# A third tile for the mixed rows, and exponentials built one channel at a time, in a kernel of a 3x3 convolution and a Laplace layer

## The chip, the cores and the metric

The kernel runs on one core of one Trainium2 chip. The metric is the device time of one execution in microseconds (us), taken as the median of several runs. Everything is float32.

## The reference

Input x has 16 images of 16 channels of 256 x 256. Two layers follow one another, each as x + L(norm(x)), where norm is a group norm over 8 groups of two channels without weights:

```python
x = x + conv3x3_circular(group_norm(x))          # written with FFTs in the reference
x = x + laplace(group_norm(x))

# laplace(x), per batch b, input channel i, output channel k:
alpha = fft2(x)
A  = 1 / (omega1 - pole1)        # [freq_y, i, k, 4]
Bm = 1 / (omega2 - pole2)        # [freq_x, i, k, 4]
S  = einsum('ikpq,oikp,xikq->oxik', residue, A, Bm)
x1 = ifft2(einsum('biox,oxik->bkox', alpha, S)).real
D  = einsum('biox,oikp,xikq->bikpq', alpha, A, Bm)
r2 = einsum('bikpq,ikpq->bkpq', D, residue)
E1, E2 = exp(pole1 * ty), exp(pole2 * tx)
x2 = einsum('kbpq,bipz,biqx->kizx', r2, E1, E2).real
return x1 + x2 / (256 * 256)
```

What matters below are the mixing (for each frequency pair a 16 x 16 complex matrix S takes the channels of alpha to the channels of the result) and the exponentials E1 and E2.

## The kernel before

The work runs in four stages, one after the other on one core.

1. *Convolution* (to about 595 us): statistics of x, the 3x3 convolution as small matmuls on TensorE (PE), and on the side the tables of A for the y frequencies (among them ct, by way of cD in HBM).
2. *Spectrum* (to about 1195 us): each image is folded along y and x and transformed by matmuls; the result goes to aD in HBM, and projections of it (D) are summed in proj.
3. *Mixing* (to about 1870 us), the stage that the change is about.
4. *Back transform* (to the end): loads of mixed rows (yk), matmuls along x and y, the transient x2 added, and the sum written out.

**The mixing loop** (lines 1222 to 1245) has 32 passes g of four steps n. One pass handles four x frequencies; its mixing matrices are in a tile sg of 32 KB per partition, of which there are two, so that pass g mixes with one while the other is filled for g + 1. A step does, in this order:

- `sums(n, w_now)`: 32 small matmuls that build a quarter of the next pass's matrices from ct and the weight tile w (line 1032), into two of four PSUM banks.
- a new tile yt (line 1228) from the pool `yp`, which has two buffers of 8 KB.
- `spread`: two copies on ScalarE (ACT, line 1049) and two shuffles on VectorE (DVE, line 1052) from PSUM to the next sg.
- four times `mix` (line 1120): 16 matmuls into one PSUM bank, and its eviction to yt (line 1233), three on ACT and one on DVE, or two and two in the step after one in which the exponentials put work on ACT.
- `store` (line 1134): four DMAs of 128 KB from yt to yD in HBM; and `load` (lines 1102, 1107): none, four, four and four DMAs (of 256 KB for n = 1, half of these ahead of the store) that bring the next pass's rows of aD into the tiles abd, which the step has just used up. All of them are issued by SyncE (SP).
- one step of `weights(g + 2)` (line 895): DVE builds v in three steps, and at n = 2 GpSimd (POOL) makes the weight tile w from it (line 930). The sums of the next pass's step 0 are the first to read it.
- one step of the generator `exps` (from g = 1 on).

All of it is emitted inside `tc.manual_schedule()`: every engine issues its instructions in the order in which they are written here. A tile of a pool that lands on bytes of an earlier tile waits for the users of those bytes (`reuse_waits="tile"`), and so does a new tile for the users of the one whose buffer it takes.

**The exponentials** (`make_exps`, lines 1161 to 1214) come in 16 pairs of channels, 8 for E1 and 8 for E2. A pair takes seven steps of the generator, with tiles of 128 x 512 (2 KB per partition), one buffer each: s_th, s_rn, s_tmp and s_ex. On POOL: the products of time and pole (two instructions of 256), then the reduction to one turn (three instructions for rn at lines 1181 to 1184, and three times a product in s_tmp and a subtraction, lines 1190 and 1191), then two that clamp. ACT makes the exponential into s_ex at the end of the third step and the sine in the fifth; POOL multiplies and folds in the sixth; SP stores s_ex to eD in the seventh.

```python
for c in (c1, c2, c3):
    nc.gpsimd.tensor_scalar(tmp, rn, float(c), None, ALU.mult)
    nc.gpsimd.tensor_tensor(th, th, tmp, ALU.subtract)
    if c == c2:
        yield
```

Ahead of the loop `first_sums` fills the first sg, and `finish_projections` turns the projections into o2 with the constant jmat. In the last pass (g = 31) there are no sums; `unmix_first` mends the rows of frequency 0 in HBM, and the first loads of stage 4 wait for the stores.

The functions that the change touches follow.

Of the kernel before, what the change touches and what calls it, by code (L numbers as in the profile page):

```python
# [9 lines left out]
FP = mybir.dt.float32  # L10
AF = mybir.ActivationFunctionType
ALU = mybir.AluOpType
# [4 lines left out]
B = 16  # L17
C = 16
N = 256
P = 128  # L20
PI = float(np.pi)
# [3 lines left out]
def conv_then_laplace_kernel(ctx: ExitStack, tc: tile.TileContext, a: dict, out: bass.AP):  # L25
# [15 lines left out]
    nc = tc.nc  # L41
    x = a["x"]

    cp = ctx.enter_context(tc.tile_pool(name="const", bufs=1))
# [6 lines left out]

    later_loads = []

    def const(name, shape):
        t = cp.tile(shape, FP, name=name, tag=name)
        later_loads.append((t, a[name]))
        return t

    cols = const("cols", [P, 24])
    kmask = const("kmask", [P, C])  # L60
    fold2 = const("fold2", [P, 2, 64])
    o2 = cp.tile([P, B, 2, 16], FP, name="o2", tag="o2")
    proj = cp.tile([P, 2, B, 16, 2], FP, name="proj", tag="proj")
    jmat = cp.tile([P, 3, P], FP, name="jmat", tag="jmat")

    def pitched(name, rows, row, *split):

# [5 lines left out]
    for b in range(B // 4):  # L73
        t = dp.tile([P, C, 8 * N + 256], FP, name=f"vD{b}", tag=f"vD{b}")
# [20 lines left out]

    ptab = ExitStack()
    tp = ptab.enter_context(tc.tile_pool(name="tables", bufs=1))
    vmr = tp.tile([P, 2, B, C], FP, name="vmr", tag="vmr")


# [54 lines left out]
    own = m16[:, 0:C:2]  # L155
    load_consts()
    halves[1] = [load_x(1, h) for h in range(2)]
    nc.sync.dma_start(out=jmat, in_=a["jmat"])
    ones = tp.tile([P, P], FP, name="ones", tag="ones")
    nc.vector.memset(ones, 1.0)  # L160
    tiny = wp.tile([P, 8], FP, name="tiny", tag="tiny")
# [557 lines left out]
    def pool(stage, name, bufs=1, **kw):  # L719
        return stage.enter_context(tc.tile_pool(name=name, bufs=bufs, reuse_waits="tile", **kw))  # L720
# [11 lines left out]
    u0 = pool(p1, "u0")  # L732
# [151 lines left out]
    m0, m1, nm0 = cols[:, 0:1], cols[:, 1:2], cols[:, 9:10]  # L884
# [10 lines left out]
    def weights(g):  # L895

        shape = [P, 32, 4]
        u = up["u" if g else "u0"].tile([P, 4, 32, 4], FP, name="u", tag="u")  # L900
        w, den, e, f = (u[:, j] for j in range(4))
        pr2, pre, pim = (prU[:, j].unsqueeze(2).to_broadcast(shape) for j in range(3))
        nc.vector.tensor_tensor(
            w,
            omg[:, g].unsqueeze(1).to_broadcast(shape),
            pims.unsqueeze(2).to_broadcast(shape),
            ALU.subtract,
        )
        nc.vector.tensor_tensor(den, w, w, ALU.mult)
        nc.vector.tensor_tensor(den, den, pr2, ALU.add)  # L910
        yield
        nc.vector.reciprocal(den, den)

        nc.vector.scalar_tensor_tensor(e, w, m1, pre, ALU.mult, ALU.add)
        nc.vector.scalar_tensor_tensor(f, w, nm0, pim, ALU.mult, ALU.add)
        yield
        v = up["v"].tile([P, 32, 2, 4], FP, name="v", tag="v")
        nc.vector.tensor_tensor(v[:, :, 0], e, den, ALU.mult)
        nc.vector.tensor_tensor(v[:, :, 1], f, den, ALU.mult)
# [10 lines left out]
        nc.gpsimd.tensor_tensor(  # L930
            w4,
            v2.unsqueeze(2).to_broadcast(full),
            m4.unsqueeze(1).unsqueeze(3).to_broadcast(full),
            ALU.mult,
        )
        return wt
# [7 lines left out]
    for u in range(len(units) + 1):  # L944
        at = units[u] if u < len(units) else None
        if at is not None:
            now = vq
            t = lp.tile([P, 2, 4, 3, P], FP, name="t", tag="t")
# [32 lines left out]
    ptab.close()  # L981


    yp = pool(p2, "yt", 2)
    g0 = pool(p2, "sg0")
    a0 = pool(p2, "abd0")
    wp = pool(p2, "w", 2)
    ep = pool(p2, "exps")
    up["u"] = pool(p2, "u")
    a1 = pool(p2, "abd2")  # L990
    zp = pool(p2, "between")
    tp = pool(p2, "ct")
    a2 = pool(p2, "abd3")
    g1 = pool(p2, "sg1")
# [10 lines left out]
        z.tile([P, 4, 4, 16, B], FP, name=f"abd{j}", tag=f"abd{j}") for j, z in ((2, a1), (3, a2))  # L1005
    ]

    zp.tile([P, 384], FP, name="between", tag="between")
# [45 lines left out]
    def first_sums():  # L1054
# [27 lines left out]
            load(0, jq)  # L1082
        return sg, w1

    def finish_projections():


        for ro in range(2):
            ps = pm.tile([P, B, 16], FP, name="ps_o", tag="ps_mix")
            nc.tensor.matmul(ps, lhsT=jmat[:, 0], rhs=accs[:, ro], start=True, stop=False)  # L1090
            nc.tensor.matmul(ps, lhsT=jmat[:, 2 - ro], rhs=accs[:, 1 - ro], start=False, stop=True)
            nc.vector.tensor_copy(o2[:, :, ro], ps)

    def load(g, jq, rows=range(4)):

# [65 lines left out]
    def make_exps(which):  # L1161


        pl = ep.tile([P, C, 2], FP, name="s_pl", tag="s_pl")
        nc.sync.dma_start(out=pl, in_=a[f"pole_e{which + 1}"])
        t = ep.tile([P, N], FP, name="s_t", tag="s_t")
        nc.sync.dma_start(out=t, in_=a[("ty", "tx")[which]].to_broadcast([P, N]))
        sign, phase, turns = (cols[:, 2 + 3 * which + j : 3 + 3 * which + j] for j in range(3))
        pim = ep.tile([P, C], FP, name="s_pim", tag="s_pim")
        for _ in range(4):  # L1170
            yield
        nc.gpsimd.tensor_scalar(pim, pl[:, :, 1], sign, None, ALU.mult)
        for q in range(8):
            th = ep.tile([P, 2, N], FP, name="s_th", tag="s_th")
            rn = ep.tile([P, 2, N], FP, name="s_rn", tag="s_rn")
            tmp = ep.tile([P, 2, N], FP, name="s_tmp", tag="s_tmp")
            ex = ep.tile([P, 2, N], FP, name="s_ex", tag="s_ex")
            for j in range(2):
                i = 2 * q + j
                nc.gpsimd.tensor_scalar(th[:, j], t, pim[:, i : i + 1], None, ALU.mult)  # L1180
            nc.gpsimd.tensor_scalar(rn, th, 1.0 / (2 * PI), turns, ALU.mult, ALU.add)
            magic = 1.5 * 2.0**23
            nc.gpsimd.tensor_scalar(rn, rn, magic, None, ALU.add)
            nc.gpsimd.tensor_scalar(rn, rn, magic, None, ALU.subtract)
            yield
            c1 = 6.28125
            c2 = float(np.float32(1.93500518798828125e-3))
            c3 = 2 * np.pi - c1 - c2
            for c in (c1, c2, c3):
                nc.gpsimd.tensor_scalar(tmp, rn, float(c), None, ALU.mult)  # L1190
                nc.gpsimd.tensor_tensor(th, th, tmp, ALU.subtract)
                if c == c2:
                    yield
            nc.gpsimd.tensor_scalar(th, th, phase, 3.1415925, ALU.add, ALU.min)
            nc.gpsimd.tensor_scalar(th, th, -3.1415925, None, ALU.max)
            for j in range(2):
                i = 2 * q + j
                nc.scalar.activation(ex[:, j], t, AF.Exp, scale=pl[:, i, 0:1])
            yield True
            yield  # L1200
            nc.scalar.activation(th, th, AF.Sin)
            yield True
            nc.gpsimd.tensor_tensor(th, th, ex, ALU.mult)
            for op, eo in ((ALU.add, 0), (ALU.subtract, 1)):
                nc.gpsimd.tensor_tensor(
                    ex[:, :, eo * P : eo * P + P], th[:, :, 0:P], th[:, :, N - 1 : P - 1 : -1], op
                )
# [11 lines left out]
    finish_projections()  # L1219
    unmix = None  # L1220
    exps, late = chain(make_exps(0), make_exps(1)), None
    for g in range(32):
# [33 lines left out]
    ep = pool(p3, "et")  # L1256
# [3 lines left out]
    up = pool(p3, "ud", 2)  # L1260
# [150 lines left out]
    u = combine(0, yk, 1)  # L1411
# [12 lines left out]
    for n, (k, b0) in enumerate(units):  # L1424
# [9 lines left out]
        if n + 1 < len(units):  # L1434
# [3 lines left out]
            u = combine(units[n + 1][1], yk)  # L1438
# [171 lines left out]
```

## Time and profile before

| what | us |
|---|---|
| median of 3 runs | 2617.32 |
| the runs | 2607.34, 2626.05, 2617.32 |
| the profiled execution | 2623.94 |
| its span in the trace | 2622.1 |
| PE busy, share of the span | 2468.6, 94% |
| DVE busy | 1980.8, 76% |
| ACT busy | 1432.6, 55% |
| POOL busy | 1290.5, 49% |
| mixing loop, first sums (1218.09) to the last pass (1835.10) | 617.0 |

All times in the views are counted from the start of the span. A row of a timeline has start, duration, engine, line, operation, tile written and read, shapes, how many instructions are merged into it, and in brackets the idle time of the engine before it and what ended that. A row of a group has line, engine, operation, tiles and shapes, then busy us and mean ns of one, then the idle time before them and its causes. PE stands for matmuls, PEld for the loading of weights beside them.

### The profile page before, as it was taken

Reading aid. Unit: us, or ns where it says so; the run is one execution under the profiler, and the core shown is the slowest. Engines: PE = TensorE matmul, PEld = TensorE weight load, DVE = VectorE, ACT = ScalarE, POOL = GpSimd, SP = SyncE. Lnnn points to the kernel's source line nnn. Section 1 sums busy time; section 2 is a strip of 40 time slices with the busy share of each in tenths; the row PEclk is TensorE's granted clock in tenths of the full one; section 3 lists DMA queues with packets and bytes.
Section 4 is the critical chain, followed back from the end, with each engine's and each line's share of the span. In section 5 each row is a group of like instructions: output and inputs, shape, how many; then the busy total and the mean of one; then the engine's idle time right before and its main releaser. Section 6 shows DMA issues by size and latency. Waiting matters only on the chain.

```text
span 2622.1 us, 84262 instructions
## 1 busy us (share of the span) xinstructions
PE 2468.6 (94%) x35314; PEld 1885.3 (72%) x35314; DVE 1980.8 (76%) x3772; ACT 1432.6 (55%) x2599; POOL 1290.5 (49%) x1179
## 2 busy tenths in 40 slices
PE   5998999989999999998999999999799999999998
PEld 2444455567777777775878778788688888888887
DVE  7777788848888888887877878887276676667666
ACT  2565566666666666665666656666244444444443
POOL 1333378433333333333666645766555565555553
PEclk9999999989999999999999999999899999999999
DMA  7888878854655655655777777777988888888884
GB/s 274 276 279 282 294 270 294 297 211 177 240 195 209 242 220 194 245 225 190 225 229 214 226 225 222 222 227 228 253 302 289 291 292 279 299 289 287 291 287 174
DMA packets 318011, 653.17 MB, mean 249 GB/s; under 512 B 49174, under 2 KB 163990, under 8 KB 305728
## 3 DMA queue, kind: packets, MB, share of 16 engines
q1 hardware_dynamic: 316464, 640.57, 72.4%
q8 instruction: 278, 4.55, 0.7%
q0 software_dynamic: 896, 3.02, 0.4%
q10 hardware_dynamic: 272, 4.19, 0.4%
q14 instruction: 101, 0.83, 0.1%
HBM read 368.15 MB, written 280.36 MB: 247 GB/s over the span
## 4 chain that ended last, share of the span: by engine, by line
PE 58%; DVE 7%; DMA 4%; SPq 3%; ACT 3%; POOL 2%; issue 1%; ACTq 0%; DVEq 0%; POOLq 0%
PE ps_mix L1120 9%; PE ps_y L777 9%; PE ps_y L785 8%; PE ps_p L1361 7%; PE ps_f L1385 7%; PE ps_f L1386 7%; PE ps_x L820 5%; DMA yD<-yt 4%; PE ps_s L1032 2%; SPq L1134 2%; PE ps_h L1345 2%; PE psd L805 1%; DVE r L1394 1%; DVE ol L1396 1%; DVE ol L1397 1%
## 5 line engine op out<-in xcount | busy, mean ns | idle before, releaser
L1120 PE MATMUL ps_mix<-abd,sg 128*64 128x128 f32 x8192 | 482.2, 276 | 39.4 <-DMA yD<-yt 16.6
L1120 PEld LDWEIGHTS ps_mix<-abd,sg 128*64 128x64 f32 x8192 | 451.9, 138 | 92.9 <-ACT yt L1233 55.7
L1325 POOL TENSOR_TENSOR u<-yk 128x512 f32<-128x512 f32 (+1 forms) x268 | 358.2, 1369 | 314.7 <-PE ps_p L1361 249.1
L305 PE MATMUL ps_conv<-xt,wc 32*32 32x512 f32 x12288 | 445.6, 602 | 36.0 <-issue 26.1
L305 PEld LDWEIGHTS ps_conv<-xt,wc 32*32 32x32 f32 x12288 | 251.1, 103 | 217.6 <-issue 127.0
L793 ACT ACTIVATE t<-ps_y,vmr 128x384 f32<-128x384 f32 x512 | 297.1, 580 | 161.1 <-PE ps_y L785 161.1
L1052 DVE STREAM_SHUFFLE sg<-ps_s 128x512 f32<-128x512 f32 (+1 forms) x264 | 329.1, 1316 | 0.0
L777 PE MATMUL ps_y<-tabE,vq 128*128 128x256 f32 x1024 | 313.2, 388 | 11.0 <-DVE vq L766 9.4
L785 PE MATMUL ps_y<-tabO,vq 128*128 128x256 f32 x1024 | 305.9, 380 | 0.0
L275 POOL TENSOR_TENSOR pair<-pair,far 128x1024 f32<-128x1024 f32 x64 | 151.7, 2370 | 304.1 <-DVE pair L272 207.7
L1385 PE MATMUL ps_f<-pt,inv 128*128 128x256 f32 x1008 | 300.4, 380 | 0.0
L1386 PE MATMUL ps_f<-hs,ey 128*128 128x256 f32 x1008 | 299.8, 379 | 0.0
L1361 PEld LDWEIGHTS ps_p<-inv,u 128*128 128x128 f32 x2048 | 268.9, 193 | 35.4 <-POOL u L1329 10.9
L1389 DVE TENSOR_TENSOR r<-ps_f,q 128x256 f32<-128x256 f32 x256 | 107.0, 418 | 241.9 <-ACT q L1388 241.9
L1361 PE MATMUL ps_p<-inv,u 128*128 128x128 f32 x2048 | 276.2, 278 | 9.8 <-POOL u L1329 9.7
L1049 ACT ACTIVATE sg<-ps_s,mcol 128x512 f32<-128x512 f32 (+1 forms) x264 | 179.3, 689 | 192.2 <-DVE sg L1052 117.1
L777 PEld LDWEIGHTS ps_y<-tabE,vq 128*128 128x128 f32 x1024 | 189.6, 191 | 87.5 <-ACT q L833 51.2
L1388 ACT COPY q<-ps_f 128x256 f32<-128x256 f32 x256 | 95.4, 373 | 274.7 <-PE ps_f L1386 250.4
L1363 ACT COPY pt<-ps_p 128x512 f32<-128x512 f32 x256 | 151.5, 592 | 134.9 <-PE ps_p L1361 134.9
L765 POOL TENSOR_TENSOR vq<-vf 128x512 f32<-128x512 f32 x64 | 81.4, 1272 | 291.6 <-DVE vf L769 281.5
L785 PEld LDWEIGHTS ps_y<-tabO,vq 128*128 128x128 f32 x1024 | 195.4, 191 | 26.9
L1233 ACT COPY yt<-ps_mix 128x512 f32<-128x512 f32 x352 | 184.1, 592 | 55.8 <-DMA yD<-yt 42.2
(237 smaller groups left out, 3993.6 us busy)
## 6 DMA issues: line engine op xcount, KB each, us to landing
xt<-in_x SPq DMA_DIRECT2D x288, 258.0 KB
vD<-pair SPq DMA_DIRECT2D x256, 256.0 KB
yD<-yt SPq DMA_DIRECT2D x512, 128.0 KB
vl<-vD SPq DMA_DIRECT2D x128, 512.0 KB
out_y<-ol SPq DMA_DIRECT2D x128, 512.0 KB
s<-vD SPq DMA_DIRECT2D x126, 512.0 KB
aD<-spec SPq DMA_DIRECT2D x15, 4096.0 KB
yk<-yD SPq DMA_DIRECT2D x60, 1024.0 KB
```

The lines of the kernel that those rows point to most:

```text
L305: nc.tensor.matmul(acc[r][32 * c : 32 * c + 32], lhsT=ready[b][0][rows, phase, tap], rhs=halves[b][u // 2][rows, q : q + 5 : 4, 2 - tap : ...
L777: nc.tensor.matmul(ps[:, 0:N], lhsT=vf[:, xo, 0, j], rhs=tabE[:, 0 : i + 2 : i + 1], start=True, stop=False, skip_group_check=True,)
L785: nc.tensor.matmul(ps[:, P : P + N], lhsT=vf[:, xo, 1, j], rhs=tabO[:, i : C + 1 : C - i], start=False, stop=True, skip_group_check=True,)
L793: nc.scalar.activation(t[:, xo, j].rearrange("p l n -> p (l n)"), ps[:, 0:384], AF.Copy, scale=vmr[:, 0, b0 + j, i : i + 1],)
L1049: nc.scalar.activation(to[..., k : k + 2], src[odd], AF.Copy, scale=nsgn)
L1052: nc.vector.stream_shuffle(to[..., C + k : C + k + 2], src[1 - odd], swap)
L1120: nc.tensor.matmul(ps[64 * t : 64 * t + 64, j], lhsT=sg[:, f : f + 2].rearrange("p f m -> p (f m)"), rhs=abd[jq][:, :, 2 * t + cc, 2 * jj ...
L1233: (nc.vector.tensor_copy if m >= (2 if late else 3) else nc.scalar.copy)(o, src)
L1325: nc.gpsimd.tensor_tensor(u[:, :, j].rearrange("p b (c n) -> p c b n", c=8), in0, in1, o)
L1361: nc.tensor.matmul(ps[:, at], lhsT=u[:, n], rhs=tab, start=True, stop=True)
L1385: nc.tensor.matmul(ps[:, e], lhsT=tab, rhs=pt[:, e], start=True, stop=False)
L1386: nc.tensor.matmul(ps[:, e], lhsT=ey[:, e], rhs=hs, start=False, stop=True)
```

## The change

It gives yt a third buffer of 8 KB, and finds the room for it in other tiles:

- s_rn and s_tmp shrink to 128 x 256 (1 KB each). The reduction therefore runs for one channel of the pair after the other, with nine instructions each instead of nine for both; the first two steps of the generator now hold one channel each, and all three products of c1, c2 and c3.
- In `weights`, f is written over w, so that u has three parts instead of four.
- o2 is made in the bytes of proj; jmat is loaded at the start of the mixing stage into the buffer of s_ex; kmask and fold2 move to the pool of the tables, which is given up after stage 2; the empty tile "between" of the mixing stage goes.

```diff
-    o2 = cp.tile([P, B, 2, 16], FP, name="o2", tag="o2")
-    jmat = cp.tile([P, 3, P], FP, name="jmat", tag="jmat")
...
+    kmask = const("kmask", [P, C], tp)
+    fold2 = const("fold2", [P, 2, 64], tp)
...
-    nc.sync.dma_start(out=jmat, in_=a["jmat"])
...
-        u = up["u" if g else "u0"].tile([P, 4, 32, 4], FP, name="u", tag="u")
-        w, den, e, f = (u[:, j] for j in range(4))
+        u = up["u" if g else "u0"].tile([P, 3, 32, 4], FP, name="u", tag="u")
+        w, den, e = (u[:, j] for j in range(3))
...
-        nc.vector.scalar_tensor_tensor(f, w, nm0, pim, ALU.mult, ALU.add)
+        nc.vector.scalar_tensor_tensor(w, w, nm0, pim, ALU.mult, ALU.add)
...
-    yp = pool(p2, "yt", 2)
+    yp = pool(p2, "yt", 3)
...
-    zp = pool(p2, "between")
...
+    jmat = ep.tile([P, 3, P], FP, name="jmat", tag="s_ex")
+    nc.sync.dma_start(out=jmat, in_=a["jmat"])
+
     def finish_projections():
+        o2 = cp.tile([P, B, 2, 16], FP, name="o2", tag="proj")
...
             th = ep.tile([P, 2, N], FP, name="s_th", tag="s_th")
-            rn = ep.tile([P, 2, N], FP, name="s_rn", tag="s_rn")
-            tmp = ep.tile([P, 2, N], FP, name="s_tmp", tag="s_tmp")
+            rn = ep.tile([P, N], FP, name="s_rn", tag="s_rn")
+            tmp = ep.tile([P, N], FP, name="s_tmp", tag="s_tmp")
             ex = ep.tile([P, 2, N], FP, name="s_ex", tag="s_ex")
             for j in range(2):
                 i = 2 * q + j
                 nc.gpsimd.tensor_scalar(th[:, j], t, pim[:, i : i + 1], None, ALU.mult)
-            nc.gpsimd.tensor_scalar(rn, th, 1.0 / (2 * PI), turns, ALU.mult, ALU.add)
             magic = 1.5 * 2.0**23
-            nc.gpsimd.tensor_scalar(rn, rn, magic, None, ALU.add)
-            nc.gpsimd.tensor_scalar(rn, rn, magic, None, ALU.subtract)
-            yield
...
-            for c in (c1, c2, c3):
-                nc.gpsimd.tensor_scalar(tmp, rn, float(c), None, ALU.mult)
-                nc.gpsimd.tensor_tensor(th, th, tmp, ALU.subtract)
-                if c == c2:
-                    yield
+            for j in range(2):
+                z = th[:, j]
+                nc.gpsimd.tensor_scalar(rn, z, 1.0 / (2 * PI), turns, ALU.mult, ALU.add)
+                nc.gpsimd.tensor_scalar(rn, rn, magic, None, ALU.add)
+                nc.gpsimd.tensor_scalar(rn, rn, magic, None, ALU.subtract)
+                for c in (c1, c2, c3):
+                    nc.gpsimd.tensor_scalar(tmp, rn, float(c), None, ALU.mult)
+                    nc.gpsimd.tensor_tensor(z, z, tmp, ALU.subtract)
+                yield
```

More of the change, by code (lines that the diff above doesn't have):

```diff
@@ L52, in conv_then_laplace_kernel, with const @@
     later_loads = []
-    def const(name, shape):
-        t = cp.tile(shape, FP, name=name, tag=name)
+    def const(name, shape, home=cp):
+        t = home.tile(shape, FP, name=name, tag=name)
         later_loads.append((t, a[name]))
@@ L59, in conv_then_laplace_kernel @@
     cols = const("cols", [P, 24])
-    kmask = const("kmask", [P, C])
-    fold2 = const("fold2", [P, 2, 64])
-    o2 = cp.tile([P, B, 2, 16], FP, name="o2", tag="o2")
     proj = cp.tile([P, 2, B, 16, 2], FP, name="proj", tag="proj")
-    jmat = cp.tile([P, 3, P], FP, name="jmat", tag="jmat")
     def pitched(name, rows, row, *split):
@@ L918, in weights @@
         nc.vector.tensor_tensor(v[:, :, 0], e, den, ALU.mult)
-        nc.vector.tensor_tensor(v[:, :, 1], f, den, ALU.mult)
+        nc.vector.tensor_tensor(v[:, :, 1], w, den, ALU.mult)
         if g == 0:
@@ L1006, in conv_then_laplace_kernel @@
     ]
-    zp.tile([P, 384], FP, name="between", tag="between")
     ct = tp.tile([P, 4, 8, N], FP, name="ct", tag="ct")
@@ L1092, in finish_projections @@
             nc.vector.tensor_copy(o2[:, :, ro], ps)
+        return o2
     def load(g, jq, rows=range(4)):
@@ L1218, in conv_then_laplace_kernel @@
     ahead, wt = first_sums()
-    finish_projections()
+    o2 = finish_projections()
     unmix = None
```

## The prediction

> **What bounds the kernel now.** I read the busy lines of the page first, then its chain (section 4), then the stretches. The change acts in the mixing stage alone, from about 1195 to 1870 us; there the chain names ps_mix matmuls (9%), "DMA yD<-yt" (4%) and SP's issues of that store (2%). So I cut out the loop, from its first sums at 1218.09 to the first matmul of the last pass (g = 31) at 1835.10: 617.0 us for 31 passes of 4 steps. Busy times in nearly that stretch (us, then PE, weight loads, DVE, ACT, POOL, clock, DMA share, GB/s):
>
> ```profile
> 1226.00:1835.00 609.00, 578.20 (x11746) 490.05 (x11742) 493.21 (x881) 396.84 (x662) 378.32 (x288) 0.99 0.77 224
> ```
>
> PE is busy 95%, POOL only 62%, DMA 77%. An average hides what matters here, so next comes PE's timeline. Undisturbed, a step (32 sums, 64 mixing matmuls) takes 4.67 us; the third start below is 0.11 us late. The last row is a step that waited 3.17 us for a store, and ran slowly after it:
>
> ```profile
> 1751.86 1.09 PE L1032 MATMUL ps_s<-ct,w 64*32 64x256 f32 x32
> 1752.88 3.71 PE L1120 MATMUL ps_mix<-abd,sg 128*64 128x128 f32 x64
> 1756.64 1.10 PE L1032 MATMUL ps_s<-ct,w 64*32 64x256 f32 x32
> ...
> 1378.35 6.64 PE L1120 MATMUL ps_mix<-abd,sg 128*64 128x128 f32 x64 [3.17 <-DMA yD<-yt]
> ```
>
> The floor of the loop is 124 steps x 4.67 = 579.1 us; 37.9 us are lost. The waits between 1215 and 1850 us (total, times, longest) say to what:
>
> ```profile
> POOL w L930 <- DVE v L919: 188.2, 24, 17.9
> ACT yt L1233 <- DMA yD<-yt: 31.9, 27, 4.0
> PE ps_mix L1120 <- DMA yD<-yt: 16.6, 12, 3.2
> PE ps_mix L1120 <- DMA abd<-aD: 2.8, 3, 2.1
> ```
>
> So nearly all of the loss is the slot of yt that is still being stored. POOL's 188 us of waiting for DVE look like room; two further timelines say how much there is. POOL, around one weight tile w (L930) and the next:
>
> ```profile
> 1734.54 1.89 POOL L930 TENSOR_TENSOR w<-v,mcol 128x1024 f32<-128x1024 f32 x1 [5.58 <-DVE v L919]
> 1736.41 1.83 POOL L1180 TENSOR_SCALAR s_th<-s_t,s_pim 128x256 f32<-128x256 f32 x2
> 1738.35 0.69 POOL L1181 TENSOR_SCALAR s_rn<-s_th,cols 128x512 f32<-128x512 f32 x1
> ...
> 1751.14 2.01 POOL L1194 TENSOR_SCALAR s_th<-s_th,cols 128x512 f32<-128x512 f32 x1
> 1753.23 1.49 POOL L1195 TENSOR_SCALAR s_th<-s_th 128x512 f32<-128x512 f32 x1
> 1754.69 1.89 POOL L930 TENSOR_TENSOR w<-v,mcol 128x1024 f32<-128x1024 f32 x1
> ```
>
> In this pass POOL has no idle time: one pair of exponentials runs from 1736.41 to 1754.72, and w follows at once. w ends at 1756.58, and the sums that need it start at 1756.64. POOL is full in such a pass. SP, in a stretch in which PE waits for nothing:
>
> ```profile
> 1565.88 2.53 SPq L1107 DMA_DIRECT2D abd<-aD  x4
> 1568.52 3.15 SPq L1134 DMA_DIRECT2D yD<-yt  x4
> ...
> 1587.79 2.73 SPq L1134 DMA_DIRECT2D yD<-yt  x4
> 1590.62 1.23 SPq L1102 DMA_DIRECT2D abd<-aD  x2
> ```
>
> From 1565.88 to 1590.62 SP issues 36 transfers with no pause, 0.687 us each. The loop has 31 x 28 of them and 24 for the exponentials, 892, which is 613 us at this rate: SP is as full as PE, and the stores are late because their issues are.
>
> **The skill against the trace.** Two pages bear on this. The Trainium skill, "GPSIMD Engine Reference", section 3.1, says that each GpSimd instruction pays a dispatch in software beside its work per element; section 4.1 calls one-input work roughly line-rate. The trace (mean ns) agrees with the first and not with the second:
>
> ```profile
> L1191 POOL TENSOR_TENSOR s_th<-s_th,s_tmp 128x512 f32<-128x512 f32 x48 | 61.5, 1281 | 4.0
> L1180 POOL TENSOR_SCALAR s_th<-s_t,s_pim 128x256 f32<-128x256 f32 x32 | 29.3, 926 | 0.8
> L1183 POOL TENSOR_SCALAR s_rn<-s_rn 128x512 f32<-128x512 f32 x16 | 24.0, 1498 | 1.4
> L1205 POOL TENSOR_TENSOR s_ex<-s_th 128x256 f32<-128x256 f32 x32 | 22.7, 731 | 1.3
> ```
>
> Half the width costs 57 to 62%, and the one-input form is the dearer; I go by these rows. "TensorE: Matmul & The Clock Gate", Part 1, says that PE falls back to half clock after an idle window of about 3.4 us. The row at 1378.35 agrees in kind (3.17 us idle, then 6.64 us instead of 3.71), as does a gap of 3.27 us at 1561.40 (then 5.38); after 2.10 us of idling at 1798.23 the step took its 3.71. The forecast goes by these three.
>
> **The change part by part.**
>
> *Third yt tile.* A step's store is issued 2 to 5 us after its last eviction and lands some 2 to 5 us later, while two tiles leave about 6 us (two steps less the time of the four evictions). Three leave about 10.8. This takes away nearly all of the 37.9 us as waits for the slot. It takes nothing from SP: between 600 and 613 us of issues remain, and a store can now lag one step more, which puts the loads queued behind it on SP later by as much. So alone it would bring the loop to some 600 to 610 us. In the last pass the evictions of step 3 wait for a matmul group that starts at 1854.76, after 8.20 us of idle time, because step 2's evictions waited for step 0's store, landed at 1854.12. With a third tile it is step 3's evictions that wait for this store, with their matmuls long done; SP's last store issue moves from 1863.4 to about 1859.8 (unmixing stores to 1855.4, two stores of 2.0 us and gaps). Gain 3.6 us, and as much for the loads of the next stage, which wait for that store.
>
> *Exponentials channel by channel.* Before, the reduction of a pair is nine instructions of 512: start to start 0.78 + 2 x 1.58 + 3 x (1.57 + 1.37) = 12.8 us. After, 18 of 256. With 0.08 us between dependent instructions (the timeline's gaps): 0.65 for the first (0.57, between half of 0.69 and all of it), 5 x 0.99 (0.91, just under L1180), 3 x 0.81 (0.73, L1205) = 8.03 per channel, 16.1 per pair: +3.3 us. Bounds: half of each 512 row plus gaps, +0.7; 0.99, 0.75 and 0.61 us, +4.3. Products ahead (1.9) and clamps behind (3.6) stay. The pair up to its sine takes 18.3 + 3.3 = 21.6 us.
>
> Behind these on POOL stands w, and PE waits for w. From one w's end POOL has 4 x 4.67 - 1.89 = 16.8 us, and 1.42 us of slack before the sums want the next (1736.43 to 1737.86): 18.2 us. The 18.3 of now is the 0.11 us late start seen above. The generator takes seven steps per pair and a pass gives four, so in 8 of the passes (g = 4, 6, 11, 13, 19, 21, 26, 28) all three working steps fall between two w: late by 3.4 us. In two (g = 9, 24) the last products of one pair (2.9) and both channels of the next do: 21.6 - 3.6 + 2.9 = 20.9, late by 2.7. In all other passes there is room. Sum 8 x 3.4 + 2 x 2.7 = 32.4 us (low 7, high 42). PE idles over 3.1 us in most of the eight; counting five, at the mean of 2.93 and 1.67, adds 11.5 us for the clock.
>
> *Edits with no cost.* jmat's load moves to behind ct on SP, where the next loads start 35 us later (ct 1173.61, abd 1209.20). f in place of w is the same DVE instruction. o2 in proj's bytes waits for DVE's own sum. Tiles that move by up to 8 KB at the stage's start and end meet other tiles; those I followed (memset of pair: the last lines matmul, 1190.5, against 1190.19; first yk, vl, et) wait for what they needed anyway. If not, some us at each boundary: bound 0 to 5.
>
> **Sum.** Loop: 579.1 + 32.4 + 11.5 + 7 for loads and SP's lag that remain = 630, against 617.0: +13. End of the stage -3.6. Together +9.5 on 2623.94 (span 2622.1 and 1.8 around it): 2633. The profiled execution stands 6.6 above the median 2617.3, so 2627 there, +0.4%.
>
> **Rivals.** (1) *Cheap halves:* if half a width costs half, w is late by 0.8 us in eight passes (6.6 us in all), SP is the bound at 600 to 610, and the change gives 7 to 17 us and 3.6: about 2601. For it: POOL's durations are rough. Against: the four rows above. (2) *Slower, by the late w:* at 0.99 us for a one-input half, w comes 4.4 us late in the eight and 3.7 in the two, every gap trips the clock (10 x 2.3), and the loop takes 579 + 42 + 23 + 7 = 651: +34 - 4 = 2648. It decides from about 4 us of lateness. Against: 0.99 is above L1180. (3) *No effect of the slot:* SP was the bound all along, the lag only grows by a step and the wait becomes "DMA abd<-aD"; with the late w hidden behind SP's lag the loop stays at 617, 2615 to 2620.
>
> **How the numbers follow.** Forecast 0.6, rival 1 0.17, rival 2 0.15, rival 3 0.08. About 1% (26 us) is what can be told from no change here. Faster by over 1% would need SP's issues to shrink too: 0.06, out of rival 1. Slower by over 1%: rival 2 and the edge of the forecast, 0.2. Range 2597 to 2653, which reaches to rivals 1 and 2; the forecast's own is 2612 to 2640.
>
> **What would show it.** L1190 and L1191 at about 0.9 and 0.73 us; the yt waits for the store nearly gone; "PEld ps_s <- POOL w" with some 10 waits of about 3 us, where it has 0.9 us now; slow matmul groups after them; SP still without pauses. Wrong if w's waits are under 1 us each, or if the loop's 4.67 us step grows outside the ten passes.

## The result, and the profile after

The changed kernel takes 2633.31 us (median; 2625.51 to 2640.03), beside 2617.02 us for the kernel before in the same series (2607.34 to 2628.43): a ratio of 1.006, 95% interval 1.0047 to 1.0074. It is slower, by about 0.6%. The profiled execution took 2632.76 us (span 2630.9), against 2623.94 (2622.1): its span is 8.8 us longer. That divides into -0.9 us up to the loop, +9.7 in the loop (626.7 us instead of 617.0) and 0.0 from the start of the last pass to the end (787.0 us in both). The medians are 16.3 us apart; where the other 7.5 us lie is not seen in these two executions. A single execution isn't fine enough for it: over all kernels below the loop starts between 1215.0 and 1225.7 us, though little ahead of it differs, so I read differences of a few us in the loop, not in the span.

Busy times in the loop of the changed kernel (us, then PE, weight loads, DVE, ACT, POOL, clock, DMA share, GB/s), in nearly its whole length:

```profile
1226.00:1843.00 617.00, 581.59 (x11714) 491.42 (x11712) 494.32 (x880) 394.85 (x660) 409.85 (x432) 0.98 0.75 221
```

PE works hardly longer than before (581.6 us; 578.2), in a stretch that is longer, and POOL is busy 410 us instead of 378. The waits between 1215 and 1850 us (total, times, longest):

```profile
POOL w L927 <- DVE v L916: 168.1, 20, 18.7
...
PEld ps_s L1027 <- POOL w L927: 28.5, 10, 3.1
...
PE ps_s L1027 <- POOL w L927: 26.1, 10, 2.8
...
PE ps_mix L1120 <- DMA yD<-yt: 7.7, 6, 2.8
...
ACT yt L1233 <- DMA abd<-aD: 1.8, 1, 1.8
```

"ACT yt <- DMA yD<-yt", 31.9 us before, is gone, and so is DVE's 15.1: no eviction waits for its slot. In their place PE waits ten times for the weight tile w, 2.6 us on average. POOL in one of these ten passes (start, duration, line, operation, in brackets the idle time):

```profile
1634.87 1.89 POOL L927 TENSOR_TENSOR w<-v,mcol 128x1024 f32<-128x1024 f32 x1 [12.50 <-DVE v L916]
1636.76 1.83 POOL L1180 TENSOR_SCALAR s_th<-s_t,s_pim 128x256 f32<-128x256 f32 x2
1638.69 0.48 POOL L1187 TENSOR_SCALAR s_rn<-s_th,cols 128x256 f32<-128x256 f32 x1
...
1656.33 1.49 POOL L1195 TENSOR_SCALAR s_th<-s_th 128x512 f32<-128x512 f32 x1
1657.79 1.89 POOL L927 TENSOR_TENSOR w<-v,mcol 128x1024 f32<-128x1024 f32 x1
```

The pair now runs from 1636.76 to 1657.82, 21.1 us where it was 18.3, and w leaves POOL at 1659.68. PE beside it:

```profile
1653.21 3.71 PE L1120 MATMUL ps_mix<-abd,sg 128*64 128x128 f32 x64
1659.74 1.96 PE L1027 MATMUL ps_s<-ct,w 64*32 64x256 f32 x32 [2.81 <-POOL w L927]
1661.63 4.40 PE L1120 MATMUL ps_mix<-abd,sg 128*64 128x128 f32 x64
1665.96 1.09 PE L1027 MATMUL ps_s<-ct,w 64*32 64x256 f32 x32
```

The sums start 0.06 us after w, after 2.81 us of idling, and then the clock is low for a while: 1.96 us for 1.09, 4.40 for 3.71. SP in the same pass:

```profile
1654.13 1.92 SPq L1134 DMA_DIRECT2D yD<-yt  x4
1656.15 3.03 SPq L1107 DMA_DIRECT2D abd<-aD  x4
1661.60 2.36 SPq L1134 DMA_DIRECT2D yD<-yt  x4
```

It has a pause of 2.4 us before 1661.60, which it doesn't have in the stretch that the prediction shows: while PE waits for w, SP catches up. The groups on POOL, forms kept apart (busy us, mean ns, idle before):

```profile
L1191 POOL TENSOR_SCALAR s_tmp<-s_rn 128x256 f32<-128x256 f32 x96 | 82.4, 858 | 8.2
L1192 POOL TENSOR_TENSOR s_th<-s_th,s_tmp 128x256 f32<-128x256 f32 x96 | 70.7, 736 | 8.0
...
L1187 POOL TENSOR_SCALAR s_rn<-s_th,cols 128x256 f32<-128x256 f32 x32 | 15.6, 486 | 3.3
```

From the starts of all 124 steps I made an account of the loop. A step's excess over its 4.67 us is either a late start of the sums, a late start of the mixing after them, or slow matmuls:

| us | before | after | forecast of after |
|---|---|---|---|
| 124 steps of 4.67 | 579.1 | 579.1 | 579.1 |
| sums at n = 0 late, for w | 0.2 | 26.8 | 32.4 |
| low clock after a wait | 4.6 | 10.8 | 11.5 |
| mixing at n = 0 late | 26.8 | 9.9 | 7, for loads and SP's lag |
| mixing at n = 3 late | 5.1 | 0.0 | (the line above) |
| small excesses | 1.2 | 0.1 | |
| loop | 617.0 | 626.7 | 630 |

So the loop after is much as forecast, and the loop before was misread. Of the 37.9 us lost before, 26.8 were lost at the mixing of n = 0. A mixing matmul reads sg and abd and writes one of four PSUM banks; it never touches yt. At n = 0 it can lack the last quarter of sg, a bank that has not been evicted, or abd, whose first two quarters (the "pair", four transfers) are loaded at n = 1 of the pass before. In the kernel before, SP and then PE around such a step:

```profile
1306.13 2.89 SPq L1102 DMA_DIRECT2D abd<-aD  x2
1309.12 2.02 SPq L1134 DMA_DIRECT2D yD<-yt  x4
1311.18 2.38 SPq L1102 DMA_DIRECT2D abd<-aD  x2
```

```profile
1314.27 1.09 PE L1032 MATMUL ps_s<-ct,w 64*32 64x256 f32 x32
1316.91 3.71 PE L1120 MATMUL ps_mix<-abd,sg 128*64 128x128 f32 x64 [1.55 <-DMA yD<-yt]
```

The last pair load is issued by 1313.56 and has landed at 1316.56, by the increments of its semaphore; the mixing starts 0.35 us later, at 1316.91. In each of the 20 passes (before the last) in which the mixing at n = 0 is over 0.25 us late, it starts 0.14 to 0.44 us after the last pair load has landed; sg was complete and the bank evicted at least a quarter of a us before that landing. So the name "yD<-yt" is a wrong label. All of SP's transfers in the loop share eight semaphores in turn, stores and loads alike, and a wait on one of them is put down to the wrong transfer. Counted from the end of step n = 1, the four pair loads have landed after 10.95 us (median over the passes) in the kernel before; the matmuls want them after 10.30.

The slot does reach PE, by way of the banks: in the six late steps at n = 3 the mixing starts some 0.05 us after the eviction of the first bank. In three of them (2.7 us) that eviction began as the slot came free; in the other three ACT was still at a copy for sg, though the slot had come free 0.1 to 0.8 us before. At n = 0 late evictions lie under the pair's delay; with the pair in time they would have cost some 5.7 us (an estimate, from their ends). So of the 37.9 us at most about 11 could be the slot's.

### The profile page after: what moved, and what is told of

The parts are those of the page before. It is cut to its first block, busy times and chain, and to the rows that moved or that the text cites. A ratio compares the mean times of both kernels' runs of the same rounds, so it can differ in the third digit from the quotient of the medians.

```text
span 2630.9 us, 84342 instructions
## 1 busy us (share of the span) xinstructions
PE 2474.7 (94%) x35314; PEld 1895.1 (72%) x35314; DVE 1984.2 (75%) x3772; ACT 1434.1 (55%) x2599; POOL 1320.7 (50%) x1323
## 4 chain that ended last, share of the span: by engine, by line
PE 56%; POOL 9%; DVE 7%; DMA 2%; SPq 2%; issue 1%; ACT 1%; DVEq 0%; ACTq 0%; POOLq 0%
PE ps_y L774 9%; PE ps_y L782 8%; PE ps_mix L1120 8%; PE ps_p L1361 7%; PE ps_f L1385 7%; PE ps_f L1386 7%; PE ps_x L817 5%; PE ps_s L1027 2%; POOL s_tmp L1191 2%; POOL s_th L1192 2%; PE ps_h L1345 2%; PE psd L802 1%; DVE r L1394 1%; DVE ol L1396 1%; POOL w L927 1%
## 5 line engine op out<-in xcount | busy, mean ns | idle before, releaser
L302 PEld LDWEIGHTS ps_conv<-xt,wc 32*32 32x32 f32 x12288 | 257.9, 104 | 208.2 <-issue 120.2
L774 PE MATMUL ps_y<-tabE,vq 128*128 128x256 f32 x1024 | 313.3, 388 | 11.2 <-DVE vq L763 9.6
L1361 PE MATMUL ps_p<-inv,u 128*128 128x128 f32 x2048 | 276.5, 278 | 11.5 <-POOL u L1329 11.4
L1386 PEld LDWEIGHTS ps_f<-hs,ey 128*128 128x128 f32 x1008 | 191.6, 190 | 26.0
```

The costliest lines, as they stand in the source:

```text
L302: nc.tensor.matmul(acc[r][32 * c : 32 * c + 32], lhsT=ready[b][0][rows, phase, tap], rhs=halves[b][u // 2][rows, q : q + 5 : 4, 2 - tap : ...
L774: nc.tensor.matmul(ps[:, 0:N], lhsT=vf[:, xo, 0, j], rhs=tabE[:, 0 : i + 2 : i + 1], start=True, stop=False, skip_group_check=True,)
L1361: nc.tensor.matmul(ps[:, at], lhsT=u[:, n], rhs=tab, start=True, stop=True)
L1386: nc.tensor.matmul(ps[:, e], lhsT=ey[:, e], rhs=hs, start=False, stop=True)
```

## The experiments

"The theory" is at first that of the prediction without its step on the slot: w is late in ten passes and costs what the account says. The question is what the third tile is worth. The loop times are from one profiled execution each, the ratios are to the kernel before, run in turn on the same chip.

**e1: the changed kernel with two tiles.**

```diff
-    yp = pool(p2, "yt", 3)
+    yp = pool(p2, "yt", 2)
```

> The changed kernel with two yt tiles again, all else kept: the exponentials still go channel by channel. It prices the third tile beside the late weight tile. Theory (the late w, ten times some 2.7 us in the loop, is the whole loss, and the third tile is worth the waits that it took from the old loop): w is late as often as in the changed kernel, and the slot's waits come back on top, since they fall in other passes than the late w: loop 640 to 650 us against 626.7, 2645 to 2655 in all. Rival (the third tile does next to nothing, SP's issues are what the loop waits for, and a late w gives SP the time to catch up): loop 627 to 632, 2633 to 2638 in all.

Measured: 2640.58 us, ratio 1.0075 (1.005 to 1.01), loop 624.4. The interval overlaps that of the change (1.0047 to 1.0074), and the loop is 2.3 us shorter than with three tiles, below both expectations and nearer to the rival. Evictions wait for the slot again; the mixing at n = 3 is late by 5.6 us once more, and less time at low clock (by 4.5 us) and a little less waiting for w make up for that:

```profile
PE ps_s L1027 <- POOL w L927: 23.4, 10, 2.8
...
ACT yt L1233 <- DMA yD<-yt: 21.5, 21, 4.1
...
DVE yt L1233 <- DMA yD<-yt: 13.2, 12, 3.6
...
PE ps_mix L1120 <- DMA yD<-yt: 6.9, 8, 1.5
```

**e2: the changed kernel without the reduction** (of lines 1185 to 1193 only the two yields stay).

```diff
             for j in range(2):
-                z = th[:, j]
...
-                    nc.gpsimd.tensor_tensor(z, z, tmp, ALU.subtract)
                 yield
```

> The changed kernel without the reduction of the angles on POOL (rn and tmp are never made, so the sines are wrong); three tiles, and w is never late. It shows what the third tile is worth alone. Theory (SP is full): the loop comes down from 626.7 to 600 to 608 us and no further, SP still without pauses, some waits at the first mixing of a pass left; 2607 to 2615 in all. Rival (PE is the bound once the slot and w are out of the way): loop 582 to 590 us, 2588 to 2598 in all.

Measured: 2626.61 us, ratio 1.0007 (0.9995 to 1.002), loop 616.0. PE no longer waits for w at all, and the loop only falls back to what it was before the change. My 2607 to 2615 us, with a loop of 600 to 608, was missed.

**e3: all the work, with cheaper forms.** On POOL the one-operation form with a constant is dear, so each gets a second operation that does nothing:

```diff
-                nc.gpsimd.tensor_scalar(rn, rn, magic, None, ALU.add)
-                nc.gpsimd.tensor_scalar(rn, rn, magic, None, ALU.subtract)
+                nc.gpsimd.tensor_scalar(rn, rn, 1.0, magic, ALU.mult, ALU.add)
+                nc.gpsimd.tensor_scalar(rn, rn, 1.0, -magic, ALU.mult, ALU.add)
...
-                    nc.gpsimd.tensor_scalar(tmp, rn, float(c), None, ALU.mult)
+                    nc.gpsimd.tensor_scalar(tmp, rn, float(c), 0.0, ALU.mult, ALU.add)
```

> The changed kernel with the five one-operation instructions of the reduction written as two operations, times 1 plus the constant and times c plus 0. The same row of work (L1181 before the change) took 0.69 us for 512 where the one-operation form took 1.50. Theory: at 256 they take 0.5 to 0.6 us instead of 0.9, a pair's work up to the sine falls from about 21 to 17 to 18 us, under the 18.2 us that a pass has, the ten waits for w vanish, and the time is that of e2: 2607 to 2615. If the form is not what made that row short, 2633 as in the changed kernel.

Measured: 2626.2 us, ratio 1.001 (0.9997 to 1.0023), loop 616.5. The groups on POOL between 1215 and 1850 us:

```profile
L1191 POOL TENSOR_SCALAR s_tmp<-s_rn 128x256 f32<-128x256 f32 x96 | 39.1, 407 | 8.3
...
L1189 POOL TENSOR_SCALAR s_rn<-s_rn 128x256 f32<-128x256 f32 x32 | 13.1, 408 | 2.7
```

Each takes less than half of its 858 ns, PE waits for w nowhere, and the gain over the change ends at the same 617 us.

**e4: the reduction spread over four steps of the generator instead of two**, in its original forms; the pair still takes seven steps, and no pair has all its work between two w. In part(j, k), j is the channel; k = 0 makes rn, k = 1 to 3 is one product and its subtraction.

```diff
-            for j in range(2):
...
+            for work in (((0, 0),), ((0, 1), (0, 2), (0, 3)), ((1, 0), (1, 1)), ((1, 2), (1, 3))):
+                for jk in work:
+                    part(*jk)
+                yield
```

> The changed kernel with the same POOL instructions in another place: a pair's reduction is spread over five steps of the generator instead of three (about 4 us each), sine and fold one step later, the store at the start of the next pair. No four steps in a row hold more than 17.5 us of POOL work. Theory (only the place of w behind the exponentials on POOL's queue costs time): the waits for w vanish though POOL does as much work as in the changed kernel, 2607 to 2615. Rival (POOL's additional work itself slows the loop, by its share of the ports or otherwise): the waits go and the steps grow, 2625 or more.

Measured: 2624.91 us, ratio 1.0017 (1.0 to 1.0033), loop 617.7. The waits:

```profile
PE ps_mix L1120 <- DMA yD<-yt: 26.8, 18, 2.6
...
ACT yt L1236 <- DMA yD<-yt: 4.0, 5, 1.8
```

With the slot out of the way and w never late, PE's waits at the mixing have grown from 16.6 us before to 26.8. e2, e3 and e4 are three ways to take the late w away; all give 616 to 618 us. So the third tile alone gains nothing in this loop, and the expectation of 2607 to 2615 us in all, taken from the prediction's 600 to 610 for the loop, fell three times. The new theory is the prediction's third rival: SP is the bound. It issues 892 transfers in the loop of the kernel before, 0.619 us each; with the short gaps between them, and the instructions that wait for semaphores, that is 608 us. It stands idle for about 10 of the 617. (A wait of SP shows as a gap ahead of the issue and not inside it, as the 5.3 us in e6 below do.) 118 of the issues took over 0.8 us, 147 us together; why is not shown, and it may be that the transfers hold these back.

**e5: the pair loads all ahead of the store of n = 1** (on top of e3).

```diff
             if n == 1 and g < 31:
-                load(g + 1, n, (0, 1))
+                load(g + 1, n)
             store(g, n, yt)
-            if g < 31:
-                load(g + 1, n, (2, 3) if n == 1 else range(4))
+            if g < 31 and n != 1:
+                load(g + 1, n)
```

> Changed kernel with the fused forms of e3 (w never late), and in step n = 1 all four pair loads are issued ahead of the store instead of two ahead and two behind. Where the loop of e3 (616.5 us) is late at the mixing of step n = 0. Theory (SP's queue is full, the order in it only moves the wait): loop 612 to 620, the wait at n = 0 goes, at least half of it comes back at n = 1 to 3 as late loads or stores. Rival (the two pair loads behind the store are the whole wait, SP has room): the n = 0 waits of about 31 us go, loop 585 to 595, total about 25 us under e3.

Measured: 2622.25 us, ratio 1.0005 (0.9994 to 1.0016), loop 619.1. The total fits the theory, the place doesn't: the waits at n = 0 did not move to other steps, they stayed, 33.4 us. The first pair load goes out 4.3 us after the end of step n = 1 instead of 2.0, because the store of n = 0 now stands ahead of it in SP's late queue; the last lands as late as before. Here the order within the full queue was worth nothing.

**e6 and e8: the pair loads from ACT's queue**, in e3 and in the kernel before (with e5's order); **e7: e6 with two tiles.**

```diff
             if jq == 1:
-                nc.sync.dma_start(
+                (nc.scalar if g else nc.sync).dma_start(
```

> e5 with the four pair loads of each pass issued from ACT's queue instead of SP's: SP has 24 issues a pass and not 28, 768 in the loop, some 520 us. Theory (SP's issues hold the loop at 617): SP gets pauses, PE becomes the bound, loop 585 to 597, total 20 to 32 us under e3 (2595 to 2606 on the clock of the run before). Rival (the transfers themselves, or the memory, are the limit and not the issuing): loop stays at 610 or more. Second rival: ACT's issues delay its evictions and copies of sg, loop over 605 with PE waiting for ACT.

> e6 with two tiles of yt instead of three: what the third tile is worth once SP has room and w is never late. Theory (with room on SP the stores are issued early, so that two tiles suffice): within 4 us of e6 in the loop, plus up to 3 us in the last pass. Rival (the slot costs what the prediction said, up to 37.9 us, and was only covered by SP): 15 us or more above e6.

> The kernel before (two tiles, exponentials of two channels at a time) with only the four pair loads of each pass issued from ACT's queue. Theory: SP's issues were the bound of the kernel before too, so this alone takes 18 to 30 us from it, without any of the change. Rival (the slot of yt was the bound before, as the prediction had it): under 8 us.

Measured: 2741.49 us (ratio 1.0462, 1.0441 to 1.0483), 2704.49 (1.0317, 1.0294 to 1.034) and 2698.03 (1.0292, 1.0263 to 1.0321); loops 734.7, 683.6 and 686.3. The theories' numbers fell, and where a rival's came out ("610 or more" in e6) it was for another reason: a wait that I had not thought of. SP's and ACT's rows in e6:

```profile
1523.01 6.99 SPq L1134 DMA_DIRECT2D yD<-yt  x4
1530.10 2.57 SPq L1107 DMA_DIRECT2D abd<-aD  x4
```

```profile
1526.69 2.56 ACTq L1102 DMA_DIRECT2D abd<-aD  x4
```

The last of SP's four stores stands still from 1524.40 to 1529.69. It carries semaphore 102; the pair load issued at 1526.69 on ACT carries it too, and its sixteenth increment comes at 1529.68. A transfer waits until the one that last used its semaphore has landed, and with two queues sharing eight semaphores SP waits for a load of ACT's that waits for PE; the loads behind it on SP come late, and PE's mixing at n = 3 is late by 108 us in all in e6:

```profile
SPq L1134 <- DMA abd<-aD: 203.3, 33, 10.6
```

On SP alone this rule costs hardly anything: in the kernel before, none of the 892 transfers starts before the one that last had its semaphore has landed, and the median is 2.15 us after that. These three runs thus say nothing about SP's room or the slot, and why three tiles do worse than two here was not followed up.

**e9: the pair loads from POOL's queue**, behind the store of n = 1 (on top of e3).

```diff
-            if n == 1 and g < 31:
-                load(g + 1, n, (0, 1))
             store(g, n, yt)
             if g < 31:
-                load(g + 1, n, (2, 3) if n == 1 else range(4))
+                load(g + 1, n)
...
             if jq == 1:
-                nc.sync.dma_start(
+                (nc.gpsimd if g else nc.sync).dma_start(
```

> Changed kernel with the fused forms of e3, and the four pair loads of each pass issued from POOL's queue behind the store of step n = 1; POOL's transfers have semaphores of their own (111 to 118 in the trace), so no transfer of SP has to wait for one of them, as in e6 to e8. SP has 24 issues a pass. Cost on POOL from the table loads of the next stage: 4 x 0.57 = 2.3 us a pass, which the fused forms leave room for. Theory (SP's issuing holds the loop at 617): loop 583 to 600, total 15 to 32 us under the kernel before. Rival (the transfers or the memory are the limit): loop 610 or more. Second rival: POOL waits at its load for the end of step n = 1 and w comes late: waits of PE for w, loop over 600.

Measured: 2623.83 us, ratio 1.0 (0.9989 to 1.0012), loop 615.5. SP has room now, but POOL takes instructions in order:

```profile
POOL abd L1102 <- PE ps_mix L1120: 117.7, 23, 11.1
...
PE ps_s L1027 <- POOL w L927: 19.4, 16, 2.6
```

It waits at the load for the end of step n = 1, then does exponentials, and w is late again, as the second rival had it: 20.5 us in the account.

**e10: fewer loads**, two of four for the third and fourth quarter of abd (on top of e3); **e11: the same with two tiles.**

```diff
         for s in rows:
+            if g and jq > 1 and s > 1:
+                continue
```

> e3 with two of the four loads each of the third and fourth quarter of abd left out in every pass but the first (the matmuls run as before, on old data): 24 issues a pass on SP and 3.0 of 3.5 MB a pass, nothing moved to another queue. Theory (SP): loop 583 to 595. Rival (PE, slots or latency): 608 or more.

> e10 with two tiles of yt instead of three, so: what the third tile is worth when SP has room and w is never late. Theory (stores then go out early enough for two tiles): within 5 us of e10 in the loop. Rival (the slot costs what the prediction put it at): 15 to 38 us above e10, and waits of ACT and DVE yt for the store of over 30 us.

Measured: 2585.25 us (ratio 0.9859, 0.9835 to 0.9883) and 2595.94 (0.9894, 0.9874 to 0.9915); loops 582.5 and 580.5. Busy times of e10 from 1226 to 1806 us and of e11 from 1226 to 1801 us:

```profile
1226.00:1806.00 580.00, 577.25 (x11855) 489.85 (x11853) 500.44 (x890) 395.93 (x667) 342.15 (x434) 1.00 0.72 210
```

```profile
1226.00:1801.00 575.00, 574.35 (x11806) 487.21 (x11796) 499.45 (x887) 394.07 (x663) 337.94 (x432) 1.00 0.72 211
```

PE is busy over 99.5% of the time at full clock: the loop stands at its floor of 579, with three tiles and with two. The slot of two tiles is free in time once SP is: in e11, up to 1801 us, evictions wait for it 5.0 us in all, and PE for evictions 0.2 us.

```profile
ACT yt L1235 <- DMA yD<-yt: 2.8, 5, 1.0
DVE yt L1235 <- DMA yD<-yt: 2.2, 2, 1.2
```

The medians are 10.7 us apart, e11 the slower, which the loops do not show. The profiled execution is the slowest of e10 and the fastest of e11, so where the 10.7 us arise stays open, and the third tile may be worth some of it outside the loop. These runs leave out bytes as well as issues (122 MB in the loop for 137; GB/s fall only from 224 to 210, since the loop is shorter), so they show that SP's transfers are the bound; that it is their issuing and not their moving rests on SP's own rows and on e12.

**e12: e9 with the pair loads behind the exponentials of n = 1 on POOL, ahead of w.**

```diff
-            if g < 31:
+            if g < 31 and n != 1:
                 load(g + 1, n)
...
             late = g and next(exps, None)
+            if n == 1 and g < 31:
+                load(g + 1, n)
```

> e9 with the four pair loads moved in POOL's order from ahead of the exponentials of step n = 1 to behind them, and still ahead of w: POOL works on the exponentials while step n = 1 runs, instead of waiting up to 11 us for its end with w queued behind. Theory (e9 lost at POOL's wait what it gained on SP): PE's waits for w go (20.5 us in e9), loop 583 to 592, 20 to 30 us under the kernel before (ratio 0.988 to 0.992). Rival (the pair loads now leave too late in passes with much work on POOL, and PE waits for abd at n = 0): loop over 600. Second rival (transfers from two queues slow each other): loop over 605 with waits for abd at n = 2 and 3.

Measured: 2621.47 us, ratio 0.9995 (0.9981 to 1.0009), loop 617.5. The theory's number fell, and its first rival holds. (The profiled execution, 2633.86 us, is the slowest of the 22.) SP has room:

```profile
SPq L1134 <- DVE yt L1233: 104.0, 58, 3.9
```

It waits 104 us for evictions, which it never had time for before. The loss sits in eleven passes, in which POOL is still at exponentials for about 3 us or more after step n = 1 has ended. POOL, then PE, in one of them:

```profile
1490.25 1.49 POOL L1195 TENSOR_SCALAR s_th<-s_th 128x512 f32<-128x512 f32 x1
1491.69 2.25 POOL L1102 DMA_DIRECT2D abd<-aD  x4
```

```profile
1495.91 1.10 PE L1027 MATMUL ps_s<-ct,w 64*32 64x256 f32 x32 [0.54 <-POOL w L927]
1498.98 3.28 PE L1120 MATMUL ps_mix<-abd,sg 128*64 128x128 f32 x56 [1.97 <-DVE sg L1047]
```

The pair loads leave 5.65 us after the end of step n = 1 (1486.04), the last of them lands at 1498.63, and PE starts 0.35 us later, as in the kernel before, whatever the label says. Over all passes:

| kernel | last pair load issued, us after the end of n = 1 | landed | wanted | mixing at n = 0 late, sum | loop |
|---|---|---|---|---|---|
| before | 6.8 | 10.95 | 10.30 | 26.8 | 617.0 |
| e4 | 6.9 | 11.2 | 10.30 | 32.6 | 617.7 |
| e5 | 6.3 | 11.1 | 10.30 | 33.4 | 619.1 |
| e10 | 4.7 | 9.06 | 10.30 | 3.3 | 582.5 |
| e11 | 4.7 | 8.96 | 10.30 | 1.0 | 580.5 |
| e12, 19 passes | 2.0 (median) | up to 9.2 | 10.30 | 0.0 | |
| e12, the other 11 | 4.8 to 7.4 | 11.4 to 13.3 | 10.30 to 10.94 | 22.5 | 617.5 |

(Medians, but for the last two lines.) Where the pair has landed some 0.4 us before it is wanted there is no wait, whichever queue it came from; where it has not, PE waits. The other passes bear on the moving of the bytes. In three of them in a row nothing is left out (4.5 MB a pass, beside 4.4 on average in the kernel before), and PE never stands still:

```profile
1498.98:1555.00 56.02, 56.02 (x1152) 47.53 (x1153) 45.89 (x83) 36.38 (x62) 30.76 (x43) 1.00 0.79 240
```

That is three times 18.67 us, the floor of a pass, at 240 GB/s. So the transfers can be moved at PE's pace, and what holds the loop is when they are issued. In e12 the 22.5 us, 11.3 of low clock after them and 4.5 for w make up the 38 over the floor. A version that computes everything and beats the kernel before was not found; e12 with the reduction spread as in e4, so that POOL is free at every n = 1, was not tried.

## Why the prediction was right, and where it was wrong

**The late w: right.** The row of L1191 gives 0.86 us (0.91 forecast), L1192 0.74 (0.73), L1187 0.49 (0.57); the pair up to its sine 21.1 us (21.6). The ten waits fall on the ten passes named (the sums of g = 5, 7, 10, 12, 14, 20, 22, 25, 27, 29). They come to 26.8 us instead of 32.4, since two of the three pieces of the reduction were sized too dear. One sign that was named failed: SP was to stay without pauses, and it pauses where PE waits for w.

**The clock: right in size, by luck.** It cost 10.8 us, against 11.5. The forecast counted five gaps of over 3.1 us; no gap was longer than 2.8. Six gaps of 2.5 to 2.8 us brought the low clock all the same, and three of 2.7 to 2.8 did not (the last section has more on this).

**The slot: wrong.** The step that failed is "This takes away nearly all of the 37.9 us as waits for the slot", with "alone it would bring the loop to some 600 to 610 us". The three runs with w in time put it at 616 to 618, no gain. The label "DMA yD<-yt" on PE's wait was taken at its word, though a mixing matmul doesn't read yt, and the waits of ACT and DVE for the slot were real but had slack behind them: at most 5.1 us of them (n = 3) reached PE. Removing these let the pair loads come later against PE's pace (26.8 us of waits grew to 32.6 in e4), because SP was as full as ever. The prediction had read that ("SP is as full as PE") and worked out 613 us for SP's issues, and then let the loop drop below that all the same. SP's own 608 us, its long issues among them, and some 10 of waits are the 617, and the tile did not change that.

**Why the sum held nevertheless.** The forecast started from the floor of 579 and added what it saw; it did not subtract from 617. That the total came so close is partly luck: for the profiled execution it said +9.5 and +8.8 came, because +13 in the loop was +9.7 and the -3.6 at its end did not come. The 7 us for loads and SP's lag had no working behind them; 9.9 were measured. For the median it said 2627, and 2633.31 was measured. The waits for w give SP time: in the changed kernel the pair is late by 9.9 us instead of 26.8. So 26.6 us more for w and 6.2 more of low clock cost the loop only 9.7. This is the mechanism of rival 3 (the bound is SP's) with the late w of the forecast on top, and not hidden behind SP's lag as that rival had it: its 617 was passed by 9.7. Rival 1 had the wrong price for half widths, rival 2 the wrong lateness (over 4 us; the longest wait was 2.8).

**The end of the stage: wrong.** The last pass is shorter, 22.4 us instead of 25.3 (-3.6 forecast), and SP's last store issue comes 2.2 us earlier, but the end of the kernel does not: from the start of the last pass it is 787.0 us in both. "As much for the loads of the next stage" did not follow. With two tiles in e1 the last pass takes 24.3 us and the remainder is 761.5; with three in e3 it is 19.8 and 764.7. Which later wait takes the gain back was not settled.

**The skill's rows.** The Trainium skill, "DMA: Bandwidth & Descriptors", section "Issuing engines are not separate DMA queues", says that starting transfers from several engines saves only the sequencer's time, "which is usually small relative to the DMA itself". Per transfer the trace agrees: 0.62 us of SP beside 3.3 us to landing. In sum it doesn't: 892 issues all but fill SP in a loop whose DMA engines are busy 77%, and 119 of them fewer are worth 34 us (e10, which moves fewer bytes too).

## What to carry to other kernels

Ask what a waiting instruction can lack (what it reads, and what it overwrites) before you believe the label of its wait, above all where many transfers share a few semaphores. A queue that hardly ever pauses may be the bound: here a deeper buffer behind it only moved the wait, and a forecast that goes below its issues times their measured rate has to say which of them get shorter. And when a new wait appears, see who catches up during it: here two thirds of the late w were paid back by a queue that was late anyway.

## What the runs showed of the hardware

- On POOL the form of a tensor-with-constant instruction matters more than halving its length (1498 to 858 ns for one operation): at 128x256, one operation (mult or add, with no second) takes 858 ns, mult and add together 407, and two tensors 736. The Trainium skill, "GPSIMD Engine Reference", section 4.1, has one-input work roughly at line rate; here its form with one operation was slower than an instruction with two inputs, and only the fused form was faster.
- A load from POOL's queue costs POOL 0.56 us to issue, much like SP's (0.60, median), but lands later: the last of four came 5.6 us (median) after its issue in e12, 4.1 us on SP in the kernel before.
- PE's clock fell after idle gaps of 2.81 and 2.49 us (sums of 1.96 us and a mixing of 5.38 us after them), but not after others of 2.69 and 2.81 us (1.10 and 3.71 both times). The Trainium skill, "TensorE: Matmul & The Clock Gate", Part 1, has a window of about 3.4 us. The clock record of the trace shows what a shorter gap costs: in the loop of the changed kernel the low stretches start whole multiples of 3.41 us apart and last 3.41 us (one of them twice that). Two such windows around the gap before 1659.74, then two around the one before 1619.51 (columns as above; the clock is the third number from the end):

```profile
1656.29:1659.70 3.41, 0.64 (x12) 0.39 (x8) 0.58 (x2) 1.84 (x4) 3.37 (x3) 1.00 0.78 235
1659.70:1663.11 3.41, 3.37 (x46) 2.15 (x48) 3.11 (x7) 1.61 (x3) 3.22 (x4) 0.50 0.37 101
1615.33:1618.74 3.41, 1.36 (x26) 1.12 (x22) 1.99 (x3) 3.29 (x5) 3.33 (x3) 1.00 0.90 292
1618.74:1622.15 3.41, 2.65 (x62) 2.12 (x64) 1.41 (x4) 1.53 (x4) 3.19 (x4) 1.00 0.74 218
```

Both gaps are 2.81 us long. The first lies in one window but for its last 0.04 us, and the next window runs at half clock; the second is cut in two by a window's edge, and no low window follows. In this loop PE idled 2.2 to 2.8 us in the windows ahead of the six low stretches, and about 2.0 at most in all others at full clock. Over the loops of all 14 kernels the shortest idle time of a window with a fall behind it is 1.95 us and the longest without one 2.03.
